# A graph network's first layer takes its late blocks in pairs, sends them spaced, and numbers its lists on ScalarE

## The chip, the cores and the metric

The kernel runs on one core of one Trainium2 chip. The core has five engines with a queue each: PE (TensorE, matrix products into PSUM; PEld is its weight load), DVE (VectorE), ACT (ScalarE), POOL (GpSimd) and SP (SyncE). DMA transfers are issued from the queues of SP (plain ones) and POOL (gathers and scatters by row number) and run on 16 DMA engines. An engine works through its queue in order; what waits in front holds everything behind it.

The metric is device time in microseconds (us). The profile is one execution taken by the hardware profiler, with start and end of every instruction.

## The reference, cut to what matters

Four graph layers over 4096 nodes of 256 features and one 4096 x 4096 adjacency matrix that is sparse (each node has its own edge and some others, here at most 23 in a row of the lists). Each layer normalises, applies relu, and adds an attention over the node's neighbours. The first, which is the one that changes:

```python
h = jnp.maximum(_layernorm(x, axis=-1), 0.0)
x = x + _L0_gnn_ref(h, adj, L0_gnn_W, L0_gnn_a)

def _L0_gnn_ref(h, adj, W, a):            # n = 4096, heads = 4, d = 64
    Wh = (h @ W).reshape(n, heads, d)
    s_i = jnp.einsum('nhd,hd->nh', Wh, a[:, :d])
    s_j = jnp.einsum('nhd,hd->nh', Wh, a[:, d:])
    e = jax.nn.leaky_relu(s_i[:, None, :] + s_j[None, :, :], negative_slope=0.2)
    e = jnp.where((adj == 0)[:, :, None], -jnp.inf, e)
    alpha = jax.nn.softmax(e, axis=1)
    out = jnp.einsum('ijh,jhd->ihd', alpha, Wh).reshape(n, heads * d)
    return jax.nn.elu(out)
```

The second layer has one head and adds `node @ W` to its attention; its table of rows is what the end of the first layer's work writes. Layers three and four are attentions of the same kind.

## The kernel before, in words

**Sparse, by lists.** The kernel never forms the 4096 x 4096 attention. It turns each row of the matrix into a list of up to 24 node numbers, and gathers the neighbours' rows from a table in DRAM by those numbers. Rows are worked on in 32 row blocks of 128, one node to a partition.

**The lists** (`scan`, L244). Quarter rows of the matrix come in by SP, ACT casts them to 8 bit (`cast`, L268), PE turns a mark and a column number into one value in PSUM (`marks`), DVE takes the eight largest of each 256 columns (L490) and merges them to the 24 largest (`merge`, L498, L500). `number` (L502) makes node numbers of them on POOL, by two small operations at L507 and L510. Beside this runs the first layer's table (`table`: norm, relu, product with W) and its early part (`early`, L515): for two row blocks at a time the first six neighbours are gathered (12 gathers), scored, weighed and added up. The order of all this is written out by hand: `plan(engine, at, ...)` puts work into numbered steps, eight to a row block, and each engine's queue gets the steps in order. Step 8(r+1) is where POOL numbers row block r; the early part of pair j begins at step `max(4*(10+j), 4*(4*j+4))`.

**Placing.** Then all nodes are sorted by the length of their lists (`sort`), so that a block holds nodes of about the same length, and POOL scatters each row block's data into DRAM by the place of its nodes (`to_place`, L652: 32 scatters). The steps in which a place may be written are named in `scan`: `if t > halves - 6 and t not in (halves - 4, halves)`, where t is the step divided by four. `reload` (L692) reads it all back: the numbers `near` and, block by block, the rows `rx`, in which stand the node's x, the early sum, its scores and what was summed so far.

**The late part** of the first layer (`layer(0)`, L945). By `CAPS` a block has a greatest number of neighbours, from 23 (block 0) down to 3 (block 31); what the early part did not take, `CAPS[b] - 6`, is gathered here: 17 rows for block 0, 8 for block 1, down to 1, and none for nine blocks. The blocks go in the order `FIRST`, which mixes long ones with those that gather nothing. For the block at place i of the order the loop does this:

- `fill(i)`: POOL issues the gathers (`fetch`, L894) of the blocks up to four ahead, as far as the ring of row buffers has room;
- `scores` (L1060 to L1103): on DVE score, leaky relu, largest and difference, then the exponential on ACT into `s_shares`;
- `weigh` (L1142 to L1204): sum, reciprocal and shares on DVE, the node's own early sum times its share (L1180; L1133 where nothing is gathered), the gathered rows times their shares (L1194), and one PE product with the identity for each row (L1185, L1204) that adds them up in PSUM;
- for the block two before, `settle`: elu and residual (ACT at L1224 and L1225, DVE at L1235 and L1236), then the next layer's norm (L576 to L592);
- for the block three before, relu on ACT (L871), two transposes on PE (L879), a copy on ACT (L881), the product with the second layer's weights (L887);
- for the block four before, `advance`: the product is added to x (DVE, L1252), ACT copies scores and numbers beside it (L1253, L1254), and POOL sends the block's 128 rows to the second layer's table (`send`, L904).

All gathers and sends share POOL's queue, in the order in which this loop issues them. Layer 1 gathers from the table that these sends write, so its first gather comes after the last of them.

The instructions stand in the queues in the program's order here (`manual_schedule`); in the lists that holds for PE, DVE, ACT and SP, and POOL's gathers and numbers keep the program's order among themselves.

## Time and profile before

| | us |
|---|---|
| median of three runs | 1770.32 (1769.03 to 1776.56) |
| the profiled execution | 1775.77 |
| its span, first to last instruction | 1774.0 |
| last merge of the lists ends | 381.3 |
| last scatter of the placing starts | 426.56 |
| first operation of the reload on POOL | 430.08 |
| first gather of the late part starts | 432.03 |
| block 0's rows are there (first score on DVE) | 464.21 |
| last send of the first layer starts | 640.85 |
| layer 1's first gather starts | 644.08 |

Over the whole span DVE is busy 78%, POOL 66%, PE 55%, ACT 24%. A line of a timeline gives start, duration, engine, line, operation, output and inputs, and in brackets the idle time before it and what ended it ("issue" means that nothing the profile shows was waited for). A line of a group gives busy time and the mean of one in ns, then the idle time in front of it. A line of the waits gives who waited for whom: total, times, longest. A gather is busy 0.95 us on POOL and the next one starts 0.30 later.

### The profile page before, as it was taken

The numbers are of one execution on the slowest core, as the hardware profiler recorded it, in microseconds if no ns is written. First come the engines' busy times: TensorE is split into PE (matmuls) and PEld (weight loads), VectorE is DVE, ScalarE is ACT, GpSimd is POOL, SyncE is SP. The second block draws the span as 40 slices with busy tenths as digits, with TensorE's granted clock in tenths as the row PEclk, the third lists the DMA queues.
The fourth block names the chain that finished last, engine by engine and source line by source line (L and its number), as shares of the span: only waits on it lengthen the run. The fifth ranks groups of instructions, "written<-read, shape, count | busy, mean of one in ns | idle before, by whom it ended". The sixth has DMA issues, their size and how long they took to land. (4 is left out here: it accounts for less than half of the span.)

```text
span 1774.0 us, 14372 instructions
## 1 busy us (share of the span) xinstructions
PE 981.3 (55%) x2565; PEld 474.8 (27%) x2565; DVE 1377.0 (78%) x3929; ACT 425.3 (24%) x1245; POOL 1165.9 (66%) x1306
## 2 busy tenths in 40 slices
PE   4967878672476622232222167778776354555445
PEld 3612323220355411111111123334333121122112
DVE  6899889961679928888888467788876597888876
ACT  5874343200244411111111112222222000000000
POOL 1067765676667447777777477777773777777774
PEclk9999888885688865555555578998889677777777
DMA  9899878346833224444444244444443767666763
GB/s 327 285 398 338 306 256 284 105 130 206 247 94 103 64 70 123 129 132 132 129 132 130 74 114 132 132 135 134 135 133 100 212 200 210 207 208 194 207 203 116
DMA packets 121786, 309.08 MB, mean 174 GB/s; under 512 B 30900, under 2 KB 49335, under 8 KB 121688
## 3 DMA queue, kind: packets, MB, share of 16 engines
q0 software_dynamic: 66832, 203.64, 39.9%
q1 hardware_dynamic: 54856, 104.44, 16.7%
q14 instruction: 74, 0.61, 0.1%
q8 instruction: 24, 0.39, 0.1%
HBM read 272.99 MB, written 35.00 MB: 174 GB/s over the span
## 5 line engine op out<-in xcount | busy, mean ns | idle before, releaser
L894 POOL DMA_INDIRECT s_ring<-s_tab,s_near x900 | 861.5, 957 | 324.4 <-issue 183.8
L1199 PE MATMUL s_acc<-s_ring,s_ident 128*128 128x512 f32 x572 | 302.2, 680 | 112.8 <-issue 92.5
L894 POOL DMA_INDIRECT s_g<-s_tab,s_keep x192 | 183.3, 955 | 64.6 <-issue 57.5
L1199 PEld LDWEIGHTS s_acc<-s_ring,s_ident 128*128 128x128 f32 x572 | 122.5, 221 | 285.5 <-issue 231.2
L490 DVE MAX8 s_cand<-s_pt 128x8 f32<-128x256 f32 x512 | 181.7, 415 | 18.3 <-PE s_pt L488 17.8
L1194 DVE TENSOR_TENSOR s_ring<-s_ring,s_shares 128x2048 f32<-128x2048 f32 (+7 forms) x119 | 183.1, 1561 | 0.0
L887 PE MATMUL s_ps<-s_we_l,s_ht 128*128 128x264 f32 x256 | 114.7, 591 | 91.8 <-ACT s_ht L881 91.8
L879 PE MATMUL s_pht<-s_ident,s_h 128*128 128x128 f32 x128 | 34.6, 363 | 201.8 <-ACT s_h L871 201.7
L268 ACT ACTIVATE s_low<-s_raw 128x1024 fp8e4<-128x1024 int32 x128 | 134.2, 1050 | 21.1 <-DMA s_raw<-in_adj_dram 17.9
L1162 DVE SCALAR_TENSOR_TENSOR s_acc<-s_ring,s_p,s_acc 128x256 f32<-128x256 f32 x269 | 131.8, 490 | 9.4
L563 PE MATMUL s_ae<-s_g,s_ident 128*128 128x512 f32 x192 | 115.9, 700 | 38.1 <-DVE s_g L554 38.1
L483 PE MATMUL s_pt<-s_low,s_mark 128*128 128x512 fp8e4 x256 | 106.1, 414 | 33.7 <-DVE s_cand L490 13.6
L887 PE MATMUL s_ps_kv<-s_wkv,s_ht 128*128 128x512 f32 x128 | 82.7, 781 | 66.0 <-ACT s_ht L881 66.0
L582 ACT ACTIVATE s_y<-s_mv,s_eps 128x1 f32<-128x1 f32 x96 | 28.3, 294 | 378.8 <-DVE s_mv L577 378.8
L488 PE MATMUL s_pt<-s_places,s_stands 128*128 128x512 bf16 x256 | 105.0, 410 | 1.4 <-DVE s_stands L460 1.4
L1103 ACT ACTIVATE s_shares<-s_e 128x32 f32<-128x32 f32 (+8 forms) x87 | 17.5, 201 | 343.8 <-DVE s_e L1096 334.0
L887 PEld LDWEIGHTS s_ps<-s_we_l,s_ht 128*128 128x128 f32 x256 | 63.7, 275 | 122.7 <-ACT s_ht L881 112.7
L1081 DVE TENSOR_TENSOR s_ring<-s_ring,s_shares 128x2048 f32<-128x2048 f32 (+7 forms) x47 | 78.8, 1676 | 21.1 <-DMA s_ring<-s_tab,s_near 21.1
L1060 DVE TENSOR_TENSOR s_e<-s_ring,s_rx 128x8 f32<-128x8 f32 (+12 forms) x87 | 16.0, 184 | 89.9 <-DMA s_ring<-s_tab,s_near 85.9
L879 PEld LDWEIGHTS s_pht<-s_ident,s_h 128*128 128x128 f32 x128 | 18.1, 173 | 243.4 <-ACT s_h L871 230.8
L507 POOL TENSOR_SCALAR s_ids<-s_top 128x23 f32<-128x23 f32 x32 | 10.1, 316 | 109.1 <-DVE s_top L498 108.7
L1084 DVE TENSOR_REDUCE s_e<-s_ring 128x32 f32<-128x2048 f32 (+7 forms) x47 | 78.9, 1679 | 1.6
(254 smaller groups left out, 1720.2 us busy)
## 6 DMA issues: line engine op xcount, KB each, us to landing
s_raw<-in_adj_dram SPq DMA_DIRECT2D x128, 512.0 KB, 8.0
s_ring<-s_tab,s_near POOLq DMA_INDIRECT x900, 2.9
s_rx<-s_placed SPq DMA_DIRECT2D x32, 262.0 KB, 7.4
s_tab<-s_kv SPq DMA_DIRECT2D x32, 256.0 KB, 2.8
s_tab<-s_keep SPq DMA_DIRECT2D x8, 528.0 KB, 6.8
s_tab<-s_rx SPq DMA_DIRECT2D x32, 132.0 KB, 1.9
s_keep<-in_x_dram SPq DMA_DIRECT2D x8, 512.0 KB, 8.1
s_vself<-s_tab SPq DMA_DIRECT2D x32, 128.0 KB, 3.0
```

The source lines that it names most:

```text
L268: nc.scalar.activation(low[r][:, ts(h, n // 4)], raw.pop(q), AF.Copy, saturate=False, accum_out=self.sums[:, r, h : h + 1],)
L483: nc.tensor.matmul(pt, lhsT=self.mark, rhs=lo[:, ts(g, IB)], start=True, stop=False)
L488: nc.tensor.matmul(pt, lhsT=self.stands[:, g, :], rhs=self.places, start=False, stop=True)
L490: nc.vector.max(out=cand[:, g * (IB // CH) + k, :], in_=pt[:, ts(k, CH)])
L563: nc.tensor.matmul(acc, lhsT=self.ident, rhs=g[:, :, k, 0:D], start=False, stop=(k == E - 1))
L887: self.nc.tensor.matmul(ps[:, :width], lhsT=ht[:, c, :], rhs=w[:, c, :], start=(c == 0), stop=(c == KC - 1),)
L894: return self.nc.gpsimd.indirect_dma_start(out=out, out_offset=None, in_=table[:, :], in_offset=bass.IndirectOffsetOnAxis(ap=idx, axis=0),)
L1081: nc.vector.tensor_tensor(kq, kq, q.unsqueeze(1).to_broadcast([P, m, D]), ALU.mult)
L1084: nc.vector.tensor_reduce(e[:, k0 : k0 + m, :], kq.rearrange("p k (h d) -> p k h d", h=4), AX.X, ALU.add)
L1162: nc.vector.scalar_tensor_tensor(acc, g[:, k, 0:D], p[:, k, :], acc, ALU.mult, ALU.add)
L1194: nc.vector.tensor_tensor(v, v, p[:, k0 : k0 + m, :].unsqueeze(3).to_broadcast([P, m, H, D // H]), ALU.mult)
L1199: nc.tensor.matmul(both, lhsT=self.ident, rhs=g[:, k : k + 2, v0 : v0 + D], start=(k == 0 and not full), stop=(k + 2 >= G and not more),)
```

## The change

The late part becomes a function of its own, `late`, and takes 13 pairs of blocks with the same number of gathered rows, and six single blocks, in the order `LATE`. DVE, ACT and PE work on a pair with one instruction of twice the width where the operands allow it; the gathered rows' products, the statistics and the sum with the second layer's product stay one per block. Gathers are issued up to two entries of `LATE` ahead. A finished block's send is put off: it is issued after three more gathers, or when the next block is finished.

In the lists the numbers are made by two ACT operations, two steps after POOL made them; the early part's gathers begin three steps later; a place may now be written in all steps of the last stretch but four; and the constants are made ahead of the first statistics.

Layers 1 to 3 keep their instructions. Their tiles come from a pool opened after `late` closes its own, and the tile for the own row has three buffers instead of four.

```diff
-FIRST = [31, 30, 29, 28, 0] + [b for k in range(1, 14) for b in (28 - k, k)] + [14]
+LATE = [
+    (30, 31), (28, 29), (0,), (26, 27), (1,), (24, 25), (2,), (3, 4), (23,), (5, 6), (7, 8),
+    (9,), (10, 11), (12, 13), (14,), (15, 16), (17, 18), (19, 20), (21, 22),
+]
...
-        for k in range(4):
-            stats(0, k)
-        next(norms[0])
-        scaled(0)
-        *_, (self.we0, _) = first
-        cast(2)
         self.constants()
-        for g in range(1, 3):
+        for g in range(3):
             for k in range(4):
                 stats(g, k)
             next(norms[g])
             scaled(g)
             cast(2 * g + 2)
+            if g == 0:
+                *_, (self.we0, _) = first
...
-            plan("pool", 8 * (r + 1), lambda r=r: self.number(r))
+            plan("act", 8 * (r + 1) + 2, lambda r=r: self.number(r))
...
-            begin = max(4 * (10 + j), 4 * (4 * j + 4))
+            begin = max(4 * (10 + j), 16 * (j + 1) + 3)
...
-            if t > halves - 6 and t not in (halves - 4, halves):
+            if t > halves - 6 and not nt // 2 * 16 <= at < nt // 2 * 16 + 4:
...
-        ids = self.pool.tile([P, TOPK - 1], F32, name=f"s_ids_{r}", tag="ids")
-        self.in_turn(
-            nc.gpsimd.tensor_scalar(ids, self.top[:, r, 1:], MARK, MARK + n, ALU.max, ALU.min)
-        )
-        self.in_turn(
-            nc.gpsimd.tensor_scalar(
-                self.ids[:, r, 0 : TOPK - 1], ids, -1.0, MARK + n, ALU.mult, ALU.add
-            )
+        a = self.pool.tile([P, TOPK - 1], F32, name=f"s_ids_{r}", tag="ids")
+        nc.scalar.activation(a, self.top[:, r, 1:], AF.Relu, bias=self.over)
+        nc.scalar.activation(
+            self.ids[:, r, 0 : TOPK - 1], a, AF.Relu, bias=self.none, scale=-1.0
         )
...
+    def late(self):
...
+        pending, since = [], 0
+        def deliver():
+            nonlocal since
+            b = pending.pop(0)
+            self.send(self.tab[1], self.own(b), self.listed[b])
+            since = 0
+        def fill(i):
+            nonlocal at, since
+            while todo and todo[0] <= i + 2:
+                m, K = size(todo[0])
+                s = (at if at + m * K <= slots else 0) if K else 0
+                if any(s < e and b < s + m * K for b, e in held.values()):
+                    return
+                j = todo.pop(0)
+                for u, b in enumerate(LATE[j]):
+                    for k in range(K):
+                        self.fetch(
+                            ring[:, s + u * K + k, :], self.tab[0],
+                            self.near[:, b, EARLY + k : EARLY + k + 1],
+                        )
+                        since += 1
+                        if pending and since > 2:
+                            deliver()
...
+        def scores(i):
+            m, K = size(i)
+            if K == 0:
+                return
...
+            nc.vector.tensor_tensor(
+                near, gathered(i)[:, :, :, D : D + H],
+                src.unsqueeze(2).to_broadcast([P, m, K, H]), ALU.add,
+            )
+            nc.vector.scalar_tensor_tensor(near, near, 0.2, near, ALU.mult, ALU.max)
+            nc.vector.tensor_copy(e[:, :, K, :], most)
...
+            nc.scalar.activation(p, flat, AF.Exp)
...
+        def weigh(i):
...
+            nc.vector.tensor_tensor(
+                by_heads(me), by_heads(early),
+                share.unsqueeze(3).to_broadcast([P, m, H, D // H]), ALU.mult,
+            )
+            if K == 0:
+                sums[i] = me
+                return
+            acc = self.pacc.tile([P, 2, D], F32, tag="acc", name=f"s_acc_0_{i}")[:, :m, :]
+            nc.tensor.matmul(acc, lhsT=self.ident, rhs=me, start=True, stop=False)
+            g = gathered(i)
+            for u in range(m):
+                for k0 in range(0, K, AT_ONCE):
+                    k1 = min(k0 + AT_ONCE, K)
+                    v = by_heads(g[:, u, k0:k1, 0:D])
+                    nc.vector.tensor_tensor(
+                        v, v,
+                        p[:, u, k0:k1, :].unsqueeze(3).to_broadcast([P, k1 - k0, H, D // H]),
+                        ALU.mult,
+                    )
+            for k in range(K):
+                nc.tensor.matmul(
+                    acc, lhsT=self.ident, rhs=g[:, :, k, 0:D], start=False, stop=(k + 1 == K)
+                )
+            sums[i] = acc
+        def settle(i):
...
+            nc.scalar.activation(ex, acc, AF.Exp)
+            nc.scalar.activation(ex, ex, AF.Copy, bias=-1.0)
+            yield
+            nc.vector.scalar_tensor_tensor(ex, ex, 0.0, xt, ALU.min, ALU.add)
+            nc.vector.scalar_tensor_tensor(xt, acc, 0.0, ex, ALU.max, ALU.add)
+            norm = self.norms_of(pool, xt if m > 1 else xt[:, 0, :], m, f"0_{i}")
+            for _ in range(m if m > 1 else 0):
+                next(norm)
+            next(norm)
+            yield
+            rn = next(norm)
...
+            yield
...
+            ps = [self.times(ht[:, u], self.we1, W, f"1_{i}_{u}") for u in range(m)]
+            yield
+            first = LATE[i][0]
+            for u in range(m):
+                nc.vector.tensor_tensor(xt[:, u, :], xt[:, u, :], ps[u][:, 0:D], ALU.add)
+                nc.scalar.copy(part(i, 2 * D, D + W)[:, u, :], ps[u][:, D:W])
+            nc.scalar.copy(part(i, D + W, D + WL), self.near[:, first : first + m, 0:TOPK])
+            for b in LATE[i]:
+                if pending:
+                    deliver()
+                pending.append(b)
+            if not todo:
+                deliver()
+            yield
...
+        for i in range(len(LATE) + 3):
+            fill(i)
+            go_on(i - 2)
+            if i < len(LATE):
+                scores(i)
+            go_on(i - 1)
+            go_on(i - 3)
+            go_on(i - 2)
+            if i < len(LATE):
+                weigh(i)
+                del held[i]
+            go_on(i - 1)
+        while pending:
+            deliver()
...
+                with tc.tile_pool(name="s_late", bufs=2) as self.pool:
+                    self.late()
+                self.pool = ctx.enter_context(tc.tile_pool(name="s_main", bufs=2))
+                for l in range(1, 4):
+                    self.layer(l)
```

`go_on(i)` moves entry i on by one `yield` of its `settle`. So in step i, in the order of the queues: norm factors, relu and transposes of entry i-2; scores of i; exponential of i-1; the second layer's rows of i-3 with their sends; the copy and second product of i-2; weighing of i; residual and statistics of i-1.

## The prediction

> **What bounds the kernel now.** I read the span by stage first (the windows view: busy time of each engine in a stretch, then the granted PE clock, DMA share and GB/s), because the shares of the page mix stages with different limits.
>
> ```profile
> core 0: us, PE busy (x) PEld busy (x) DVE busy (x) ACT busy (x) POOL busy (x), PEclk, DMA share, GB/s
> 0.00:351.00 351.00, 254.82 (x864) 114.95 (x865) 307.33 (x927) 183.56 (x378) 181.08 (x271) 0.91 0.82 289
> 351.00:432.00 81.00, 44.12 (x101) 16.32 (x99) 42.05 (x118) 2.79 (x7) 57.40 (x68) 0.73 0.44 153
> 432.00:464.00 32.00, 4.17 (x14) 2.68 (x14) 10.05 (x47) 4.90 (x14) 23.10 (x24) 0.50 1.02 253
> 464.00:600.00 136.00, 97.46 (x333) 71.45 (x334) 116.33 (x464) 56.22 (x202) 89.61 (x92) 0.82 0.40 123
> 600.00:644.00 44.00, 24.69 (x87) 17.36 (x85) 30.12 (x128) 17.30 (x64) 8.79 (x10) 0.84 0.10 34
> ```
>
> DVE sets the pace of the lists up to 351 us. From there to 432 it is half idle and POOL is the queue that matters. In the timeline of POOL at the end of the lists each line is a start, a duration and what ended the wait before it:
>
> ```profile
> 361.41 0.31 POOL L507 TENSOR_SCALAR s_ids<-s_top 128x23 f32<-128x23 f32 x1 [2.00 <-DVE s_top L498]
> 362.51 1.08 POOL L894 DMA_INDIRECT s_g<-s_tab,s_keep  x1 [0.49 <-PE s_pt L488]
> ...
> 377.67 1.00 POOL L652 DMA_INDIRECT s_placed<-s_keep,s_pos  x1 [0.30 <-issue]
> ...
> 385.03 0.34 POOL L507 TENSOR_SCALAR s_ids<-s_top 128x23 f32<-128x23 f32 x1
> ...
> 386.75 1.08 POOL L894 DMA_INDIRECT s_g<-s_tab,s_keep  x1 [0.49 <-issue]
> ...
> 426.56 0.97 POOL L652 DMA_INDIRECT s_placed<-s_keep,s_pos  x1 [0.30 <-issue]
> 430.08 0.16 POOL L718 IOTA s_place_of<- 128x32 f32 x1 [2.55 <-DMA s_placed<-s_keep,s_pos]
> ```
>
> A gather takes a slot of 1.26 us (0.95 and 0.30 of issue), a scatter 1.28. From 351.4 to 427.5 POOL stands still only around the numbers.
>
> From 432 to 464 the reload fills the DMA engines (1.02) and DVE waits for block 0's 17 rows. From 464 the late part of the first layer runs, until layer 1's first gather at 644.08:
>
> ```profile
> 474.76 1.00 POOL L904 DMA_INDIRECT s_tab<-s_rx,s_near  x1 [0.30 <-ACT s_rx L871]
> 481.12 0.98 POOL L904 DMA_INDIRECT s_tab<-s_rx,s_near  x1 [5.35 <-ACT s_ex L1225]
> ...
> 600.89 0.98 POOL L904 DMA_INDIRECT s_tab<-s_rx,s_near  x1 [0.85 <-ACT s_rx L1254]
> 606.25 0.99 POOL L904 DMA_INDIRECT s_tab<-s_rx,s_near  x1 [4.38 <-ACT s_rx L1254]
> ...
> 640.85 0.97 POOL L904 DMA_INDIRECT s_tab<-s_rx,s_near  x1 [3.04 <-ACT s_rx L1254]
> 644.08 0.99 POOL L894 DMA_INDIRECT s_ring<-s_tab,s_near  x1 [2.26 <-DMA s_tab<-s_rx,s_near]
> ```
>
> Up to 600 POOL is nearly packed with gathers and sends, with gaps where a send waits for ACT's copies of its rows. After it only sends are left, one per block, 5.4 us apart: that is DVE's time for a small block. The waits, and DVE's groups, whose mean tells what a wider operation costs:
>
> ```profile
> POOL s_tab L904 <- ACT s_rx L1254: 37.5, 15, 5.6
> L1194 DVE TENSOR_TENSOR s_ring<-s_ring,s_shares 128x768 f32<-128x768 f32 x5 | 4.7, 947 | 0.0
> L1194 DVE TENSOR_TENSOR s_ring<-s_ring,s_shares 128x512 f32<-128x512 f32 x4 | 2.7, 680 | 0.0
> L1194 DVE TENSOR_TENSOR s_ring<-s_ring,s_shares 128x256 f32<-128x256 f32 x5 | 2.1, 412 | 0.0
> ```
>
> 256 elements more cost 0.267 us, so an operation of 256 has 0.145 us that does not grow. The many small operations (four to forty elements) start about 0.2 us apart whatever their width. That is what taking two blocks in one instruction saves.
>
> **The change, part by part.**
>
> Start of the lists. The constants (L431 to L460, 11.9 to 14.4 us) move ahead of the first statistics, into DVE's 3.83 us wait for x. But the second group's x lands at 16.05, and DVE already waits 1.70 us for it; the wait grows instead. 0 us.
>
> Numbers on ACT. 64 POOL operations (0.316 and 0.248 us) become 64 ACT ones of 23 elements; the nearest ACT row is the 128x24 cast, 0.214. ACT's queue now waits for the merge of row block r, and the casts behind it wait too. They are at least four quarter rows (eight marks, some 11 us of DVE) ahead at that point, and ACT already waits 179 us in all for DVE's scores at L542. Only from 60 to 85 us is ACT full (22.8 of 25). Bounds: 0, and 64 x 0.22 = 14 us if all of it lay on the path. I take 0.9, the two numbers in that stretch, as the rest lies in ACT's idle time.
>
> One rule speaks against this step: the Trainium skill, ScalarE: Activation LUTs, Rules for kernel authors, would give relu, min and max to VectorE and not to ScalarE. DVE is busy 307 of 351 us here and its 24-element operation takes 0.19, so by the rule 64 x 0.19 = 12 us would be added to the pacing engine, against the 0.9 of the row.
>
> End of the lists. Places may now be written in step 240 to 243 as well, so ten of them go ahead of the 12 gathers of pair 14, two behind, then pair 15's 12, then 20. From 351.44: 10 x 1.28 to 364.3, 12 x 1.26 to 379.4, 2 to 382.0; pair 15's numbers follow the last merge (381.3) by two ACT operations, to 381.9, so its gathers run to 397.1 and 20 places to 422.8, against 427.5. Pair 15's rows then need 14 us to be weighed (403.8 to 418.0 now), 413 at the latest, before their place's turn at 420. The reload starts 4.6 us earlier; bounds 0 (DVE lags and the last merge is later) and 6.
>
> Late part, DVE. 13 pairs and 6 single blocks make 19 steps (0 to 18) instead of 32. From start-to-start times a step with gathers costs: norm factors 0.8, and ahead of them a wait of 0.4 for ACT's two small operations (0.41 us of idle before 635.03 now), which now follows the statistics directly; scores 1.0 (0.9 single); adding the product 0.33 per block of step i-3; weighing 1.6 (1.25) and the products, per block, 0.08 less than the rows above; residual and statistics of step i-1, 2.8 for a pair (two at 0.72 and four of statistics, unmerged, 1.3) or 1.65. A pair at three rows each is 9.2 us, where two blocks are now 11. Steps without gathers are 4 to 5.5.
>
> Late part, POOL. Its order has 25 gathers, then the first send, which waits for step 3: block 0's products (467.1 to 471.9), its 17 matmuls of 0.46 to 478.0, the exponential on ACT behind it, and step 0's copies: 479.7. Now 32 gathers are out by then, so POOL loses 9 us here, and this decides the stretch that follows. After it a send stands after three gathers and its rows are ready; nothing waits. POOL packed (1.26, 1.29), rows usable 2.0 after (401.98 to 403.82 now), DVE as above:
>
> ```
> step (blocks)  POOL to  rows   DVE to     step      POOL to  rows   DVE to
> 2 (0)          465.7    464.2  474.6      11 (9)    544.3    546.3  554.6
> 4 (1)          465.7    468    489.8      12 (10)   553.2    555.2  562.4
> 6 (2)          491.1    493.1  502.7      13 (12)   563.4    565.4  573.1
> 7 (3,4)        508.8    510.8  518.9      14 (14)   568.5    570.5  580.4
> 9 (5,6)        525.3    527.3  534.7      16 (17)   583.7    585.7  596.1
> 10 (7,8)       536.7    538.7  547.0      18 (21)   591.5    593.5  611.4
> ```
>
> So POOL's rows are what DVE waits for up to step 13, and DVE paces the rest. Behind step 18 come its exponential, residual, norm, transposes, product and copies, 14.8 us along ACT, DVE and PE (the same way is 14.9 now, from 625.95 to 640.85): last send at 626.2, layer 1's first gather at 629.4 instead of 644.08, 14.7 less. The unknown widths (512-wide residual between 0.68 and 0.84, ACT's 512-wide exponential between 0.57 and 0.8) move this by 2 either way.
>
> Other edits. The late pool's release before layer 1 costs nothing: layer 1's first DVE work stands in front of 20 us of gathers (644 to 665). Three buffers for the own row instead of four in layers 2 and 3: PE reads it within the block; if not, a fraction of a us each. Layers 1 to 3 are otherwise the same instructions.
>
> Sum: -4.6 + 0.9 - 14.7 = -18.4. The profiled execution is 1775.77 (span 1774.0 and 1.8 around it), so 1757.4; it is 5.4 above the median of the runs, 1770.32, so I give 1752.
>
> **Rivals.**
>
> DVE alone decides (more gain). If the first send did not hold the gathers, DVE's steps would run on: 132 us from 464 to 596, then the tail: first gather at 614, -30 - 3.7, so 1736.6. For it: DVE is 0.86 busy from 464 to 600. Against: the send is ahead of 68 gathers in POOL's order, and no row there shows a send that was passed.
>
> Sends hold POOL as they do now (less gain). POOL's gaps from 464 to 600 beyond the issue time add up to 18 us now; the walk keeps 14 in one piece and no other. Half of the 18 on top, 9, gives -9.4: 1761. Against: sends are written one step later than the copies; for: single blocks' sends, and the last twelve, are not spaced.
>
> The product comes too late (slower). Now a block's exponential is asked for two blocks after its product; then, one step. If PE is late, DVE waits before the residual. Three early waits of DVE for PE are 2.64, 1.95 and 1.52 us; 2 us at each of 19 steps is 38, some 10 of it where rows are late anyway: +28 - 18.4, 1780. It decides from about 1.5 us a step. Against: PE needs about 6.5 us of a 9.2 us step (matmuls 0.68, 0.5 and 0.28), so it ends ahead.
>
> **How the numbers follow.** Forecast 0.62, more gain 0.13, less 0.16, slower 0.09. About 0.5%, 8.9 us, is what a measurement of this kernel can tell from no change, so faster is under 1761.5: the forecast but for 0.02, all of the larger gain and half of the smaller, 0.81; same 0.10; slower 0.09. The range, 1736 to 1765, takes in both gains and the bounds of the terms (2 at the end of the late part, 0 to 6 at the lists' end), and leaves out the slower rival and what the widths of the others add beyond it.
>
> **What would show it.** The reload's first POOL operation near 426, now 430.08; layer 1's first gather about 199 us after it, now 214; one gap of some 14 us in POOL ahead of the first send and none over 2 until the gathers end; DVE steps of 9 us for pairs. It is wrong if DVE waits for PE before the residual, if the casts in the lists start late (more DVE waits for PE than now, 17.8 us), or if gathers stop behind sends.

## The result, and the profile after

| | before | after |
|---|---|---|
| median | 1772.05 (1769.03 to 1776.56) | 1756.63 (1755.88 to 1757.82) |
| ratio | | 0.991, 95% interval 0.9894 to 0.9925 |
| the profiled execution, its span | 1775.77, 1774.0 | 1757.82, 1756.1 |
| first operation of the reload on POOL | 430.08 | 425.20 |
| from there to layer 1's first gather | 214.0 | 206.5 |
| from there to the end of the span | 1129.9 | 1124.4 |

The kernel is 0.9% faster, 15.4 us by the medians, and the forecast was 1752. In the two profiles the three stretches add up to -4.9 - 7.5 - 5.5 = -17.9, against -18.4 in the prediction (the profiled execution of the kernel before is one of its slower ones, so the profiles differ by more than the medians). But the prediction had them as -3.7, -14.7 and 0: the sum holds because two misses cancel, and that is luck.

Six of the twelve experiments fell on two chips on which the kernel before itself takes 2140.73 and 2123.89 us: their profiles show long waits that nothing in them explains (on POOL 86 to 103 us in waits of over 2 us without a releaser, against 0 to 13 on the other chips), so the times of those six decide nothing here, and only durations of single instructions and waits in front of POOL's sends are read from them.

The windows view of the kernel after, for the stretches that answer to those of before (busy time by engine, then granted PE clock, DMA share, GB/s):

```profile
core 0: us, PE busy (x) PEld busy (x) DVE busy (x) ACT busy (x) POOL busy (x), PEclk, DMA share, GB/s
351.00:427.00 76.00, 45.38 (x102) 17.31 (x103) 45.88 (x120) 5.37 (x15) 54.65 (x60) 0.77 0.47 163
459.00:595.00 136.00, 96.06 (x292) 61.09 (x292) 102.64 (x329) 46.28 (x146) 86.16 (x90) 0.84 0.39 116
595.00:632.00 37.00, 20.52 (x58) 12.84 (x58) 19.31 (x72) 12.97 (x40) 11.75 (x13) 0.74 0.15 52
```

DVE was busy 116.33 of 136 us in the late part and is busy 102.64 now. From block 0's first score to the last send it is 122.58 where it was 146.44: 23.9 us of DVE's work are gone, and 7.5 of them reach the end. POOL's timeline shows what took the rest:

```profile
389.52 0.94 POOL L899 DMA_INDIRECT s_g<-s_tab,s_keep  x1 [1.02 <-ACT s_keep L515]
...
425.20 0.16 POOL L723 IOTA s_place_of<- 128x32 f32 x1 [2.60 <-DMA s_placed<-s_keep,s_pos]
...
475.01 1.00 POOL L909 DMA_INDIRECT s_tab<-s_rx,s_near  x1 [15.53 <-ACT s_rx L1108]
...
598.22 1.00 POOL L909 DMA_INDIRECT s_tab<-s_rx,s_near  x1 [2.50 <-ACT s_rx L1108]
600.97 0.96 POOL L909 DMA_INDIRECT s_tab<-s_rx,s_near  x1 [1.74 <-DMA s_tab<-s_rx,s_near]
604.18 0.96 POOL L909 DMA_INDIRECT s_tab<-s_rx,s_near  x1 [2.25 <-ACT s_shares L1021]
...
625.76 0.96 POOL L909 DMA_INDIRECT s_tab<-s_rx,s_near  x1 [2.22 <-issue]
628.49 0.96 POOL L909 DMA_INDIRECT s_tab<-s_rx,s_near  x1 [1.76 <-DMA s_tab<-s_rx,s_near]
631.71 0.98 POOL L899 DMA_INDIRECT s_ring<-s_tab,s_near  x1 [2.26 <-DMA s_tab<-s_rx,s_near]
```

Three things are to be seen. The first send holds POOL for 15.53 us, with all the gathers behind it. The last sends do not follow at 1.29 us, as a gather follows a send, but at 2.7 to 3.3, and what they wait for is named in some of the brackets: the landing of the send before. And ACT's last copy of rows ends at 624.13 (it starts at 623.90 and takes 0.23), 4.4 us before the last send starts. So it looks as if the last twelve sends, and not their rows, set the end; the first experiment tries this.

DVE's waits in the late part of the kernel after (total, times, longest):

```profile
DVE s_ex L1079 <- ACT s_ex L1077: 10.3, 4, 3.8
DVE s_y L590 <- ACT s_y L588: 7.1, 18, 0.4
DVE s_e L1007 <- DMA s_tab<-s_rx,s_near: 5.9, 2, 5.6
DVE s_rx L1106 <- PE s_ps L892: 5.4, 3, 3.6
```

The third is a wait for rows that were gathered behind the sends (four more waits for rows, of 5.2 us in all, are not among these lines). The first is a wait for sums that PE has not finished when the exponential is asked for.

The last stretch, layers 1 to 3, has the same instructions in both kernels and is 5.5 us shorter. The gathers' group of the kernel before and of the kernel after (busy time and mean ns of one, idle before):

```profile
L894 POOL DMA_INDIRECT s_ring<-s_tab,s_near x900 | 861.5, 957 | 324.4 <-issue 183.8
```
```profile
L899 POOL DMA_INDIRECT s_ring<-s_tab,s_near x900 | 854.7, 950 | 322.7 <-issue 179.1
```

Each gather takes 7 ns less. From start to start of neighbouring gathers in layer 1 (the few more than 1.5 us apart left out) the mean is 1.2586 us before and 1.2508 after; 807 of the 900 gathers lie in layers 1 to 3, so 807 x 0.0078 = 6.3 us. Whether that was the change or the execution had to be tried.

### The profile page after: what moved, and what is told of

The parts are those of the page before. It is cut to its first block, busy times and chain, and to the rows that moved or that the text cites. A ratio compares the mean times of both kernels' runs of the same rounds, so it can differ in the third digit from the quotient of the medians.

```text
span 1756.1 us, 13928 instructions
## 1 busy us (share of the span) xinstructions
PE 969.4 (55%) x2476; PEld 459.5 (26%) x2493; DVE 1355.2 (77%) x3733; ACT 427.0 (24%) x1222; POOL 1140.3 (65%) x1242
## 5 line engine op out<-in xcount | busy, mean ns | idle before, releaser
L498 DVE MAX8 s_cand<-s_pt 128x8 f32<-128x256 f32 x512 | 182.2, 416 | 25.1 <-PE s_pt L496 24.1
L1350 DVE TENSOR_TENSOR s_ring<-s_ring,s_shares 128x2048 f32<-128x2048 f32 (+7 forms) x94 | 154.8, 1673 | 0.0
L586 ACT ACTIVATE s_y<-s_mv,s_eps 128x1 f32<-128x1 f32 (+1 forms) x83 | 24.5, 295 | 408.9 <-DVE s_mv L581 408.9
L892 PE MATMUL s_ps_kv<-s_wkv,s_ht 128*128 128x512 f32 x128 | 78.5, 745 | 67.5 <-ACT s_ht L886 67.5
L496 PE MATMUL s_pt<-s_places,s_stands 128*128 128x512 bf16 x239 | 99.1, 415 | 0.0
L892 PEld LDWEIGHTS s_ps<-s_we_l,s_ht 128*128 128x128 f32 x256 | 68.5, 290 | 110.6 <-ACT s_ht L1099 50.4
L1257 DVE TENSOR_TENSOR s_ring<-s_ring,s_shares 128x2048 f32<-128x2048 f32 (+7 forms) x47 | 78.8, 1676 | 21.1 <-DMA s_ring<-s_tab,s_near 21.1
L1279 ACT ACTIVATE s_shares<-s_e 128x40 f32<-128x40 f32 (+7 forms) x64 | 13.2, 206 | 327.0 <-DVE s_e L1272 317.0
L1343 PE MATMUL s_acc<-s_me,s_ident 128*128 128x512 f32 x60 | 39.3, 742 | 67.3 <-DVE s_me L1338 59.7
L1239 DVE TENSOR_TENSOR s_e<-s_ring,s_rx 128x9 f32<-128x9 f32 (+15 forms) x64 | 11.9, 187 | 79.0 <-DMA s_ring<-s_tab,s_near 74.9
```

Source lines behind the costliest of these rows:

```text
L496: nc.tensor.matmul(pt, lhsT=self.stands[:, g, :], rhs=self.places, start=False, stop=True)
L498: nc.vector.max(out=cand[:, g * (IB // CH) + k, :], in_=pt[:, ts(k, CH)])
L892: self.nc.tensor.matmul(ps[:, :width], lhsT=ht[:, c, :], rhs=w[:, c, :], start=(c == 0), stop=(c == KC - 1),)
L1257: nc.vector.tensor_tensor(kq, kq, q.unsqueeze(1).to_broadcast([P, m, D]), ALU.mult)
L1350: nc.vector.tensor_tensor(v, v, p[:, k0 : k0 + m, :].unsqueeze(3).to_broadcast([P, m, H, D // H]), ALU.mult)
```

## The experiments

Ratios are to the kernel before, run on the same chip, with their 95% intervals. The stretches of the profiles on the chips without stalls, side by side:

| kernel | numbers on | reload's first POOL op | to layer 1's first gather | to the end | ratio |
|---|---|---|---|---|---|
| before | POOL | 430.08 | 214.0 | 1129.9 | |
| before, free sends | POOL | 429.51 | 215.0 | 1128.8 | 1.0003 |
| late part alone | POOL | 430.85 | 208.3 | 1128.9 | 0.9968 |
| after, numbers back | POOL | 428.85 | 208.4 | 1131.1 | 0.9977 |
| lists alone | ACT | 416.82 | 212.3 | 1124.4 | 0.9936 |
| after | ACT | 425.20 | 206.5 | 1124.4 | 0.991 |
| after, free sends | ACT | 426.71 | 200.8 | 1123.4 | 0.9865 |
| after, free sends, more ahead | ACT | 423.92 | 191.4 | 1123.6 | 0.9823 |

### Sends that do not wait for one another

Theory A: a send waits for the landing of the one before, and this is what the late part lost. Theory B: sends follow rows that PE makes late. All sends write one table; the edit tells the program that they write different rows.

```diff
     def send(self, table, idx, in_):
-        self.nc.gpsimd.indirect_dma_start(
+        i = self.nc.gpsimd.indirect_dma_start(
...
+        if table is self.tab[1]:
+            self.after(i, self.fetched)
+            self.tc.declare_no_dep(i.ins, group="sent", reason="rows differ")
+            self.tc.add_to_no_dep_group("sent", i.ins)
```

With it, layer 1's first gather waits for all 32 sends; POOL's order is kept by the fetches on both sides of a send (three small index fills of the reload move ahead into a wait).

> The changed kernel, with one thing more: a send to the second layer's table no longer waits until the send before it has landed (the rows differ, so the writes are told apart; layer 1's first gather waits for all 32 instead). Order of all queues as it is. Theory A (each send waits for the landing of the one before: the last twelve start 2.7 to 3.3 us apart, although ACT's last copy of rows ends at 624.1 and the last send starts at 628.5; two earlier back-to-back sends cost POOL 2.6 and 2.3 us at 505 and 588): last sends 1.3 us apart, last send at about 624 on the same timeline, and 2 us earlier gathers after 505; 4 to 7 us less than the changed kernel, 1750 to 1752.5, ratio to the kernel before about 0.987 to 0.988. Theory B (the sends only follow rows that PE's products at a lower clock make late): within 1 us of the changed kernel, ratio 0.991.

Measured: 1749.98 us (1748.76 to 1752.65), ratio 0.9865 (0.9847 to 0.9883), by the medians 6.65 less than the kernel after (8.0 by the ratios, since the chips differ). The end of POOL's sends in its timeline:

```profile
622.72 0.97 POOL L921 DMA_INDIRECT s_tab<-s_rx,s_near  x1 [3.39 <-ACT s_rx L1139]
623.99 0.97 POOL L921 DMA_INDIRECT s_tab<-s_rx,s_near  x1 [0.30 <-issue]
627.48 0.98 POOL L900 DMA_INDIRECT s_ring<-s_tab,s_near  x1 [2.52 <-issue]
```

A pair's second send follows 1.27 behind the first, and what a pair waits for is now its rows (ACT L1139). The stretch is 200.8 instead of 206.5. Theory A holds, and the size is about as written.

> The kernel before, with the sends freed of one another in the same way. Theory A says the wait for the landing is new with pairs: before, a block's send comes 5.4 us after the last one and finds it landed, so at most some 2 us are won (one gap of 2.2 at 630): 1768 to 1772, ratio 0.998 to 1.000. If the sends' order were a cost of the kernel before as well, the 38 us that POOL waits in front of its sends would shrink and 5 us or more be won, ratio under 0.997.

Measured: 1774.09 us, ratio 1.0003 (0.9993 to 1.0013). Before, the same wait cost nothing; with pairs it does. The likely reason is that blocks came one at a time before.

The profile's 0.96 us of a send is not the transfer: its landing comes 2.4 us after the issue at the least, 2.6 in the median (of all 64 transfers of that line). The Trainium skill, Perfetto Trace Analysis, DMA Instruction — SWDGE (GPSIMD), says the same in general: the end that the profile shows for such an instruction is that of descriptor generation, not of the data. This trace agrees: 0.96 shown, 2.73 at the least to a next send that has to wait.

### The lists alone, the late part alone

Lists alone: the kernel before with the numbers, the steps, the places and the constants of the change.

```diff
-            plan("pool", 8 * (r + 1), lambda r=r: self.number(r))
+            plan("act", 8 * (r + 1) + 2, lambda r=r: self.number(r))
...
-            begin = max(4 * (10 + j), 4 * (4 * j + 4))
+            begin = max(4 * (10 + j), 16 * (j + 1) + 3)
...
-            if t > halves - 6 and t not in (halves - 4, halves):
+            if t > halves - 6 and not nt // 2 * 16 <= at < nt // 2 * 16 + 4:
```

> The kernel before with the edits of the lists alone: numbers on ACT two steps later, gathers of the early part three steps later, the other steps for the places, constants first (the two bias constants share a tile with eps). The late part as before. The prediction's sum gives -4.6 +0.9 = -3.7; the trace of the changed kernel has the reload's first POOL operation 4.9 us earlier: 1765 to 1769, ratio 0.996 to 0.998. If the numbers on ACT cost the pacing engine something that the places win back, it is nearer to 1.000; if the whole gain of the change were in the lists, 0.991.

Measured: 1761.1 us (1755.22 to 1765.21), ratio 0.9936 (0.992 to 0.9952). That is some 11 us, three times what I expected. In its profile 5.5 of it stands in layers 1 to 3 (1124.4 against 1129.9), which this kernel does not touch at all, and 1.7 in the late part, which is that of before. So the shorter layers are no accident of one execution: they come with the edits of the lists.

How much the lists' own stage gains stays loose. The runs of this kernel spread over 10 us, with granted clocks between 0.757 (1763.53 and 1765.21) and 0.764 (1755.22, the profiled one, whose reload starts at 416.82). In that profile PE had 0.94 from 240 to 300 us, where the kernel after had 0.89, with the same order of instructions in the lists. Why this kernel is granted more is open.

Late part alone is the reverse: the kernel after with all edits of the lists undone.

> The changed kernel with the lists as before (numbers on POOL, old steps, old order of the constants). In the profiles the stretch from the reload's first POOL operation to layer 1's first gather is 206.5 us instead of 214.0, so 7.5 less: 1762 to 1765, ratio 0.9945 to 0.9965. If the 5.5 us by which layers 1 to 3 are shorter in the profile of the changed kernel are its doing (pool, three buffers) and not the gathers' pace in that execution (1.25 us a gather against 1.26), they are here too: 1757 to 1760, ratio 0.991 to 0.994.

Measured: 1767.52 us (1766.64 to 1769.70), ratio 0.9968 (0.9955 to 0.9981), 5.7 us: nearer to the first of the two expectations, and just outside its range. Layers 1 to 3 take 1128.9, against 1128.8 and 1129.9 in the two profiles of the old late part with the old lists.

### The numbers

Which edit of the lists makes the gathers faster? The kernel after with the numbers on POOL again, and the early part's steps with them; the places, the constants and the late part stay changed.

```diff
-            plan("act", 8 * (r + 1) + 2, lambda r=r: self.number(r))
+            plan("pool", 8 * (r + 1), lambda r=r: self.number(r))
...
-            begin = max(4 * (10 + j), 16 * (j + 1) + 3)
+            begin = max(4 * (10 + j), 4 * (4 * j + 4))
```

First on a chip with stalls:

> The changed kernel with the numbers back on POOL (and the early part's steps with them); the places, the constants and the late part stay changed. Three traces with numbers on POOL have a gather every 1.258 us in layer 1, three with numbers on ACT one every 1.250. Theory A (POOL's two small operations per row block make every gather of the program slower): the slot goes back to 1.258, layers 1 to 3 are 5 to 6 us longer, the late part about 1, and the lists change by -2 to +3: 1761 to 1766, ratio 0.993 to 0.996. Theory B (the pace belongs to the execution or to something else in the change): slot 1.250, 1755 to 1759.

Measured: 2142.03 us where the kernel before takes 2140.73, so the time says nothing. Reckoned as above, a gather of layer 1 started every 1.2603 us in it, and every 1.2502 and 1.2504 in two kernels with the numbers on ACT on the same chip. Again, on a chip without stalls:

> The changed kernel with the numbers back on POOL (and the early part's steps with them), again, on a chip without the long stalls of the run before. There a gather took 1.2615 us in layer 1 with the numbers on POOL and 1.2509 with them on ACT. Theory A: numbers on POOL make each gather 7 to 8 ns slower, so layers 1 to 3 take 5.5 us longer and the late part 1, and the lists change by -2 to +3: ratio to the kernel before 0.993 to 0.997. Theory B (the lists gain by the places alone and the numbers are worth nothing): ratio 0.990 to 0.992, as the changed kernel.

Measured: 1769.72 us (1768.12 to 1773.23), ratio 0.9977 (0.9966 to 0.9988), a little above the range of theory A. The numbers, with the early part's steps, are worth 0.9977 - 0.991 = 0.0067, some 12 us, the larger part of the whole change. Its gathers' group, on the page:

```profile
L899 POOL DMA_INDIRECT s_ring<-s_tab,s_near x900 | 863.4, 959 | 323.0 <-issue 180.3
```

959 ns against 950. The table above says where the 12.3 us between the two profiles lie: 3.65 ahead of the reload, 1.9 in the late part, 6.7 in layers 1 to 3. In the lists the numbers off POOL, with their steps, bring 428.85 to 425.20. What the places and constants bring, 430.08 to 428.85, cannot be told from no gain: three kernels with the lists as they were start the reload at 429.51 to 430.85, and three with the lists of the change at 423.92 to 426.71 (the lists alone, at 416.82, stand apart).

In which gathers does the slower pace stand? The gathers of the first 15 pairs have the numbers between them, those of the last pair come just behind the last two row blocks' numbers, and all others follow. Each line below has a number of gathers, their least, median and greatest duration in ns, and the starts of the first and the last in us. The first three lines are from the kernel before; the last two are from the kernel after, where x186 takes in the first half of the last pair:

```profile
L894 POOL DMA_INDIRECT s_g<-s_tab,s_keep x180: 942/947/1210, 95.7 to 376.4; - x180
L894 POOL DMA_INDIRECT s_g<-s_tab,s_keep x12: 949/953/1083, 386.7 to 400.7; - x12
L894 POOL DMA_INDIRECT s_ring<-s_tab,s_near x900: 948/954/1336, 432.0 to 1748.0; - x180
...
L899 POOL DMA_INDIRECT s_g<-s_tab,s_keep x186: 940/946/1137, 96.3 to 387.6; - x186
L899 POOL DMA_INDIRECT s_ring<-s_tab,s_near x900: 940/946/1263, 427.1 to 1728.8; - x180
```

So the numbers do not slow the gathers that they stand between (947 in the median, against 946). The duration steps up once, between pair 14's gathers and the last pair's, and stays there to the end. All five profiles with numbers on POOL have this step at this place (946 to 949 ahead of it, 953 to 957 behind it), and none of the eight others has a step.

Does one such operation suffice? The kernel after with one more operation on POOL, once, its output unused:

```diff
         nc.gpsimd.tensor_copy(self.ids[:, :, TOPK], own)
+        spare = pool.tile([P, TOPK - 1], F32, name="s_spare", bufs=1)
+        nc.gpsimd.tensor_scalar(spare, own[:, 1:TOPK], MARK, MARK + n, ALU.max, ALU.min)
```

> The changed kernel with one POOL operation more, of the kind and size of a number's first (23 elements), once, among the constants; its output is not used. If it is enough that such an operation was run once, the gather's slot is 1.258 in layer 1 and the kernel 6 to 7 us slower, 1762 to 1764. If it has to stand between the gathers (64 of them), or the pace has another cause, the slot stays at 1.250 and the time at 1755 to 1758.

Measured on the chip with stalls: 2145.71 us, which says nothing; its gathers' group:

```profile
L901 POOL DMA_INDIRECT s_ring<-s_tab,s_near x900 | 857.1, 952 | 607.1 <-issue 295.8
```

952 ns, between the 949 and 950 of two kernels without it and the 961 with all 64, on the same chip. Start to start in layer 1 it is 1.2541, between 1.2502 and 1.2603. Neither expectation holds: with one operation, run once at the start, a third of the difference is there. But it has no step; its gathers take 949 in the median from the first pair on. And that the operation makes these 3 ns is not shown: two kernels with the same 64 operations differ as much (the late part alone has 946 ahead of the step, the kernel with the numbers back 949).

That a program with the numbers on POOL has slower gathers from the last pair on is shown by five profiles with them (956 to 961 on the page) and eight without (949 to 951), on three chips. By what means is not: whether it is the operations themselves, what stands beside them at the step, or where the program's tiles and code come to lie was not tried apart.

### The first send

The prediction says that some 14 us of POOL are lost in front of the first send, and that this decides the stretch behind it. The kernel after, with gathers up to four entries ahead, so that 44 of them stand in front of the first send and not 25:

```diff
-            while todo and todo[0] <= i + 2:
+            while todo and todo[0] <= i + 4:
```

> The changed kernel with gathers issued up to four entries ahead instead of two, so that 44 gathers stand in front of the first send instead of 25 (30, 31 and 28 are then sent one after the other). Theory A: the hold of 15.5 us is filled with gathers; last gather some 10 to 15 us earlier (593.5 now), DVE sets the pace from block 0 on, and the end is then set by the sends that follow one another at 3.2 us: 8 to 13 us less, 1744 to 1749. Theory B: the hold is slack that the end of the late part, bound by sends alone, does not see: within 2 us of 1756.6.

Measured on the chip with stalls: 2146.64 us, undecided. The hold there was 8.5 us, against 18.9 and 19.2 in two kernels that differ from it in the look-ahead and in the lists' numbers or one POOL operation. Then the same edit on top of the free sends:

> The kernel with free sends (the first experiment), with one edit more: gathers are issued up to four entries ahead instead of two, so that 44 gathers stand in front of the first send instead of 25. Theory A: the first send's hold of POOL decides the stretch behind it: with free sends DVE still waits 5.6 us at 508 and 1.4 at 562 for rows that were gathered behind it. Filled, these two waits go: 5 to 8 us less than with free sends alone, ratio to the kernel before 0.982 to 0.984 (1742 to 1745 where the kernel before takes 1773). Theory B: what DVE waits for is PE (exponentials of sums that come late, four waits of 9.9 us, and the last products, 5.2), and rows that come earlier only make these waits longer: within 1.5 us of free sends alone, ratio 0.986 to 0.987.

Measured: 1742.33 us (1740.61 to 1746.41), ratio 0.9823 (0.9806 to 0.9839), 7.65 less than free sends alone (7.4 by the ratios, since the chips differ). Its POOL goes from the gathers into the first send without a hold, and the end comes earlier:

```profile
481.77 1.35 POOL L900 DMA_INDIRECT s_ring<-s_tab,s_near  x1 [0.30 <-issue]
483.42 1.00 POOL L921 DMA_INDIRECT s_tab<-s_rx,s_near  x1 [0.31 <-issue]
...
611.86 0.97 POOL L921 DMA_INDIRECT s_tab<-s_rx,s_near  x1 [0.30 <-issue]
615.35 0.98 POOL L900 DMA_INDIRECT s_ring<-s_tab,s_near  x1 [2.52 <-issue]
```

DVE's wait for rows in this part, 5.6 and 1.4 with free sends alone, is 0.3 here after block 0's own. Theory A holds, with the sends freed; what the look-ahead alone would bring the kernel after is not shown. This is the fastest version of the study; it beats both kernels.

What holds the first send? In ACT's timeline of the kernel after, the copies of blocks 30 and 31 (L1107, L1108) stand behind block 0's exponential, which waits for 17 matmuls:

```profile
473.65 0.38 ACT L1076 ACTIVATE s_ex<-s_acc 128x256 f32<-128x256 f32 x1 [2.67 <-PE s_acc L1065]
474.06 0.42 ACT L1077 ACTIVATE s_ex<-s_ex 128x256 f32<-128x256 f32 x1
474.39 0.21 ACT L1107 COPY s_rx<-s_ps 128x8 f32<-128x8 f32 x2
```

The experiment puts them ahead of it:

```diff
-            go_on(i - 1)
             go_on(i - 3)
+            go_on(i - 1)
```

> The changed kernel with two lines of the late loop exchanged: the copies of the block three back stand on ACT ahead of the exponential of the block one back (and its addition is unmoved on DVE). Theory A: POOL's 15.5 us hold ahead of the first send is ACT's copies of blocks 30 and 31 standing behind the exponential of block 0, which waits for 17 matmuls until 473; the additions they follow end at 470.4. Then the first send starts at about 471.0 instead of 475.0, gathers follow 4 us earlier to about step 13, and the time is 2 to 4 us less: 1752.5 to 1754.5. Theory B: the hold does not decide (DVE or the sends at the end do): within 1 us of 1756.6.

> The changed kernel with two lines of the late loop exchanged, as in the run before on the other chip, where the hold ahead of the first send was 15.2 us against 18.9 and 19.2 in two kernels without the exchange. Theory A: the first send starts at 471.0 instead of 475.0 because its rows' copies no longer stand behind the exponential of block 0, and the gathers behind it follow: 2 to 4 us less than the changed kernel, ratio to the kernel before 0.987 to 0.989. Theory B: the end of the late part is set by the sends alone: ratio 0.990 to 0.992.

Measured: 2148.04 and 2125.57 us, both on chips with stalls (0.3% and 0.1% above the kernel before there), so the time is undecided. The hold was 15.2 and 13.5 us, against 18.9 to 19.2 in three kernels without the exchange. In the second one's ACT timeline the copies are done 1.9 us before the exponential starts:

```profile
535.92 0.20 ACT L1107 COPY s_rx<-s_ps 128x8 f32<-128x8 f32 x2
536.02 0.23 ACT L1108 CAST s_rx<-s_near 128x48 f32<-128x48 uint32 x1
538.16 0.38 ACT L1076 ACTIVATE s_ex<-s_acc 128x256 f32<-128x256 f32 x1 [1.91 <-PE s_acc L1065]
```

So by these two profiles ACT's order makes 4 to 6 us of the hold; the rest is that these rows are not made sooner. That the time follows was not shown.

### Sends without spacing

The kernel after, a finished pair's two sends issued at once.

```diff
             for b in LATE[i]:
-                if pending:
-                    deliver()
                 pending.append(b)
-            if not todo:
-                deliver()
+                deliver()
```

> The changed kernel without the spacing: a finished pair's two sends are issued at once, one directly behind the other, where before 19 of 32 had gathers in between. Theory A (a send that follows a send waits until that one has landed, 2.7 to 3.3 us instead of 1.29): about seven pairs' second sends now cost POOL 1.9 us more each while POOL is what DVE waits for, and the first send of a pair comes when its rows have hardly been copied: 6 to 14 us slower than the changed kernel, ratio to the kernel before 0.995 to 0.999. Theory B (the spacing is worth nothing, since the same sends wait at the end anyway): ratio 0.990 to 0.992, as the changed kernel.

Measured: 2125.64 us on a chip with stalls, ratio 1.0011 (0.9992 to 1.0031), the same as the exchange above on that chip. Ahead of the last gather, POOL's timeline has seven waits of 1.74 to 1.78 us in front of a send, as a send directly behind a send shows them; the kernel with the exchange has none of these there. All holds in that part add up to 42.4 us, against 33.5, but 5.7 of these 8.9 are the first send's hold (19.1 against 13.5), which the exchange shortens. So the waits that the spacing avoids are there; that it is worth time is not shown.

## Why the prediction was right, and where it was not

**The lists' end: right in time, not in its reason.** The places were to end at 422.8 and the reload to start near 426; the last place starts at 421.63 and the reload at 425.20. But with the numbers back on POOL the same places gain nothing that can be told from noise, so the 4.9 us need the numbers and their steps. And the last merge ends at 388.5 and not at 381.3: row block 29's merge now comes 13.2 us behind that of 28, and came 7.1 behind it (7.1 again with the numbers and the steps back). DVE's waits for PE in the lists, which were to show a late cast, are 24.1 us instead of 17.8. All this was covered: POOL had pair 15's first six gathers to do, and waited 1.02 us for the numbers.

**The first send: right.** It was to come 49.6 us after the reload's first operation (479.7 less 430.08) after some 14 us of idle POOL; it came 49.8 after it, with 15.53 idle. That this decides what follows is shown by the second of the two look-ahead runs, for freed sends. The rival in which DVE alone decides was right about what could be had (its stretch was 184, and 191.4 was reached with the hold filled and the sends freed) and wrong about this kernel.

**DVE's steps: right to a few per cent.** A pair at three rows was to take 9.2; from one step's scores to the next it is 8.8 (563.41 to 572.22). The 512-wide residual is 0.69 and ACT's exponential 0.57 to 0.61, at the low ends of their bounds. Step 18 was to end 181.3 us after the reload's first operation and ends 184.2 after it. Some of that is the wait for sums, four times, 10.3 in all, which I had excluded with "it ends ahead"; by the prediction's own words this wait was to show it wrong. That rival's mechanism was there, in four of 19 steps, and not in all.

**The tail: the term that was mis-sized.** "Behind step 18 ... 14.8 us ... last send at 626.2." The rows were ready 14.7 us behind step 18 (609.4 to 624.13), but the last send stood at 628.49, 19.1 behind it and so 4.3 late. With the 2.9 us by which step 18 itself is late, that makes the 7.2 by which the late part fell short of 14.7: layer 1's first gather comes 206.5 us after the reload's first operation and not 199. The failed step is "a send stands after three gathers and its rows are ready; nothing waits": 13 of the 32 sends have no gather between them and the send before, and stand 2.7 to 3.6 us behind it in place of 1.29. Behind the first send and ahead of the last gather POOL stands three times over 2 us in front of a send (2.61, 3.54 and 2.27, twice directly behind a send), where none was forecast. I had named this for the rival with less gain ("the last twelve, are not spaced") and did not price it from the rows of before that showed it: the send at 493.25 stood 3.24 behind its forerunner, though its rows had been copied by 488.20, and the one at 632.52 stood 3.20 behind. Freed, the sends gave 6.65 us.

**The numbers: the wrong sign.** "I take 0.9" as a cost, and 0 for layers 1 to 3, "the same instructions". Measured, the numbers' move gains some 12 us: 3.65 at the lists' end (which my -4.6 held already), 1.9 in the late part, and 6.7 in layers 1 to 3, where the instructions are the same and each gather is about 1% shorter. The trace of before does hold a hint: its first 180 gathers take 947 ns in the median, and all behind the last numbers 953 and 954. The prediction priced them all at one slot of 1.26 us. That the step would go with the numbers' move, the trace of before could not show. The rule that spoke against ACT (the Trainium skill, ScalarE: Activation LUTs, Rules for kernel authors: relu, min and max belong on VectorE) did not decide: ACT had the room. DVE in its place was not tried.

So the total came out right partly by luck: a gain that was not foreseen made up for the one that fell short. With the numbers on POOL, all the rest of the change together gains 0.23%.

## What to carry to other kernels

Transfers that write one table are ordered by it even where their rows differ: look for a send that directly follows a send, and price it at the landing (2.7 to 3.3 us here), not at the issue (1.29). When work on one engine is halved, list the in-order queues that now meet each other sooner; here POOL's first send and the last twelve let 7.5 of DVE's 23.9 us through, and with both mended the stretch is 22.6 us shorter. And when small operations leave POOL, compare the gathers far behind them too: here these changed, and not the ones between them.

## What the hardware showed unexpectedly

- A gather of the late part and of layers 1 to 3 takes 949 to 951 ns on average in eight profiles with the numbers on ACT, 956 to 961 in five with them on POOL, and 952 with one such POOL operation at the start of the program. It holds on each of the three chips that profiled both kinds in these experiments. The slower pace begins in one step, with the last pair's gathers (947 ns ahead of it, 953 behind it in the kernel before). The cause is open.
- The same program takes 1773 and 1774 us on two chips and 2124 and 2141 on two others. On the slower ones a gather lasts as long (949 ns); what is added are waits without a releaser in the profile, on POOL up to 13.6 us, on ACT up to 29.5. No experiment moved the time there by more than 0.4%. The kernel after was not run there, but five close relatives of it were, in six runs, and none was faster than the kernel before (ratios 1.0002 to 1.0032): the gain of the change was seen on the faster chips alone.
- The lists' stage goes with the granted clock: from 240 to 300 us one kernel was granted 0.94 and another 0.89 with the same order of instructions, and the first one's reload started 8 us earlier. Which of the two makes the other is open.
